# A graph layer's edge sum on one core: part of its products in two float32r parts, a 123rd row in the rank product, compares earlier

## The chip, the core and the metric

The kernel runs on one core of a Trainium2 chip. A core has a matrix engine (TensorE, PE in the profile, with its weight loads as PEld), VectorE (DVE), ScalarE (ACT), GpSimd (POOL), a queue engine SyncE (SP) that issues most transfers, and 16 DMA engines. The metric is the device time of one execution in microseconds; several executions were timed, and one more was profiled.

## The reference

A message sum over 206250 edges into 6250 nodes, a small three-layer network on each node, a residual and a layer norm. Rows have 128 float32 values.

```python
edge_aggr = jnp.zeros((n, 128)).at[src].add(edge_attr_128)       # 206250 rows into 6250
combined  = concatenate([x, edge_aggr, global_expand], -1) @ W_c + b_c
h = softplus(combined @ W1 + b1)
h = softplus(h @ W2 + b2)
out = layernorm(x + h @ W3 + b3)
```

`src` is random, so the sum is the work: each edge's row has to find its node. The sums must keep float32 accuracy; the one-hot operands of the products below are exact zeros and ones.

## The kernel before, in words

The nodes are cut into 32 buckets of 196 (`BL`). The edge rows are sorted by bucket on the chip and then summed bucket by bucket. There are eight groups of edge columns (`GROUPS`, 846 pairs of columns in all); groups 5, 6 and 7 (from `GAP` on) are called late here, and their positions are worked out in two parts.

1. *Rows.* `load_rows` (SP, `sync_dma` L293) brings 1032 KB of edge rows; `code_rows` (ACT L1114) writes a code beside each row.
2. *Positions* of a group: `count_set` (DVE L498) builds the one-hot tile `pair_ib` of the buckets of 16 columns; `counted`, `evened` and `started` make from it each bucket's first position for every four columns (a quad); `ranked` counts, for each row, the rows ahead of it: one matmul with `pair_ib` (L557, 122 rows contracted, 512 columns), and then, for each quad, a weight load and a matmul of `starts_h` (L559) that adds the bucket's start. In late groups the tile is `starts_h_late`. `slot_set` (DVE L576) takes the slot out of the result. `pair_set` and `paired` (L727, L742) give the row number in DRAM of each pair.
3. *Sort.* A piece is up to three pairs. `compare` builds its one-hot `sort_hot`: for every second piece on VectorE (L1137), for the others by six ACT operations (L1140) and a relu (L1142). `gather` (PE L1153) permutes the rows with it, fp32, 129 columns a matmul; `settle` (ACT L1165) copies PSUM into one of six `pair_sets`; `scatter_row` (POOL L1182) writes a pair of columns to the DRAM table `rows_by` with an indirect DMA, one every 1.3 us in the plan (`SCATTER`). SP also writes filler rows (`some`, the fills).
4. *Sum.* `sum_steps` reads `rows_by` back, up to eight chunks of 128 rows in a load (`chunks`, six buffers). A unit is up to four chunks of one load. `match` (DVE L990) builds the unit's one-hot `hot` (node within the bucket, 196 columns a chunk), `product` (PE L1013) multiplies it with the chunk, fp32, and `add` (DVE L1036) adds the finished PSUM part into `sums_t`.
5. *Nodes.* `node_layers` runs the network on blocks of 512 nodes (PE L1356, L1357, L1360, L1395; ACT L1367 to L1373; DVE L1381, L1403, L1406; POOL L1437). The sum steps that are left after the last gather run between its steps.

The order on PE, DVE, ACT and SP is written out by a planner inside the program: each step gets a planned time (`when`), and the sorted list is the program order of all four queues. `COMPARED`, `GATHERED`, `SETTLED` say how long ahead of a piece's first scatter its steps stand; `SPREAD` adds to that for a compare on ACT. GpSimd's scatters follow the same plan. The planned times only set the order; on the chip each instruction waits for its semaphores.

## Time and profile before

| | us |
|---|---|
| median of 3 runs (lowest, highest) | 1288.87 (1285.73, 1288.93) |
| profiled execution | 1289.92 |
| its span, first to last instruction | 1288.2 |
| mean granted TensorE clock | 0.962 |
| PE, DVE, ACT, POOL busy | 1167.7, 1027.6, 1003.9, 880.9 |
| scatters L1182, first start to last | 22.1 to 1127.0 |
| products L1013 busy | 675.1 |
| gathers L1153 busy | 498.5 |

A row of a group of instructions reads: line, engine, operation, output and input tiles, shapes, count; then busy us, mean ns of one, the idle time of its engine just ahead of them and what ended it. An fp32 matmul of the program shows as two records (L1013 has 3516 for 1758 matmuls). Durations of matmuls overlap in the pipeline, so busy time over count is below the mean of one. "issue" as a releaser is time in which the engine waited for nothing that the profile shows.

### The profile page before, as it was taken

The page shows a single profiled execution, that of the slowest core. Times are in us where ns is not written, and L with a number is a line of the kernel's source. Part 1 is how long each engine was busy: PE and PEld are TensorE (multiplying, and loading weights), DVE is VectorE, ACT ScalarE, POOL GpSimd, SP SyncE. Part 2 cuts the span into 40 slices and gives each one's busy share as a digit, 9 for nine tenths or more (in the row PEclk, how much of TensorE's full clock was granted, in tenths as well). Part 3 has the DMA queues.
Part 4 walks back from the last instruction along what each step waited for, and adds up shares of the span by engine and source line. Part 5 has one row for each costly group of instructions (what it writes and reads, how often), then busy time and mean ns, then how long its engine had stood idle before and what let it go on. Part 6 is the DMA issues. An engine that isn't in the chain of part 4 may idle for free.

```text
span 1288.2 us, 26304 instructions
## 1 busy us (share of the span) xinstructions
PE 1167.7 (91%) x8617; PEld 1111.8 (86%) x8617; DVE 1027.6 (80%) x2260; ACT 1003.9 (78%) x2335; POOL 880.9 (68%) x915
## 2 busy tenths in 40 slices
PE   5778898888998998999899999999999999899893
PEld 5667788877988898989899999999999999898772
DVE  7868977888789977899878887789876767687784
ACT  5897987899687888977998888988899999403343
POOL 2777777777577776776777777777777777750334
PEclk9788998989999998999999999999999999999996
DMA  6789998899999997997999999999999999874421
GB/s 248 240 296 347 344 334 288 305 344 355 339 327 331 362 330 278 319 325 246 322 309 309 323 336 328 345 313 335 316 350 334 369 336 363 288 218 140 140 75 53
DMA packets 174636, 381.96 MB, mean 297 GB/s; under 512 B 27546, under 2 KB 118626, under 8 KB 160670
## 3 DMA queue, kind: packets, MB, share of 16 engines
q1 hardware_dynamic: 130751, 260.70, 61.2%
q0 software_dynamic: 41328, 115.65, 23.1%
q10 hardware_dynamic: 2415, 3.85, 0.9%
q8 instruction: 72, 1.18, 0.4%
q14 instruction: 70, 0.57, 0.1%
HBM read 242.47 MB, written 142.20 MB: 299 GB/s over the span
## 4 chain that ended last, share of the span: by engine, by line
PE 65%; DVE 12%; ACT 8%; DMA 7%; issue 4%; POOL 3%; SPq 0%; ACTq 0%; DVEq 0%; POOLq 0%
PE part L1013 37%; PE sorted L1153 21%; ACT pairs L1165 4%; DMA rows_by<-pairs,pair 4%; POOL rows_by L1182 3%; ACT sort_hot L1140 3%; DMA chunks<-rows_by 3%; DVE hot L990 2%; DVE past L727 1%; PE small L557 1%; PE small L559 1%; ACT sort_hot L1142 1%; DVE sort_hot L1137 1%; DVE sums_t L1036 1%; PE small L1395 1%
## 5 line engine op out<-in xcount | busy, mean ns | idle before, releaser
L1182 POOL DMA_INDIRECT rows_by<-pairs,pair x846 | 828.1, 979 | 298.3 <-issue 202.8
L1013 PE MATMUL part<-hot,chunks 128*128 128x196 f32 x3516 | 675.1, 335 | 13.2 <-DVE sums_t L1036 9.9
L1165 ACT COPY pairs<-sorted 64x387 f32<-64x387 f32 (+2 forms) x1144 | 542.6, 474 | 118.8 <-PE sorted L1153 95.7
L1013 PEld LDWEIGHTS part<-hot,chunks 128*128 128x128 f32 x3516 | 582.0, 193 | 21.9 <-DVE sums_t L1036 11.3
L1153 PE MATMUL sorted<-rows,sort_hot 122*128 122x129 f32 x3384 | 498.5, 288 | 44.5 <-ACT sort_hot L1142 32.0
L1153 PEld LDWEIGHTS sorted<-rows,sort_hot 122*128 122x128 f32 x3384 | 457.6, 199 | 53.5 <-ACT sort_hot L1142 36.3
L990 DVE TENSOR_TENSOR hot<-chunks,both_ps 128x784 f32<-128x784 f32 (+3 forms) x541 | 426.1, 809 | 9.2 <-DMA chunks<-rows_by 9.0
L1140 ACT ACTIVATE sort_hot<-plain,slot 122x128 f32<-122x128 f32 x840 | 292.8, 394 | 18.6 <-PE sorted L1153 6.3
L1036 DVE TENSOR_TENSOR sums_t<-sums_t,part 128x392 f32<-128x392 f32 (+1 forms) x262 | 143.5, 548 | 134.0 <-PE part L1013 133.0
L1137 DVE TENSOR_TENSOR sort_hot<-slot,both_ps 122x768 f32<-122x768 f32 x143 | 134.5, 940 | 1.9 <-PE sorted L1153 1.0
L1142 ACT ACTIVATE sort_hot<-sort_hot 122x768 f32<-122x768 f32 x143 | 118.6, 830 | 3.9
L1437 POOL TENSOR_SCALAR y<-y,mv,rs 128x128 f32<-128x128 f32 x40 | 31.1, 785 | 93.8 <-DVE rs L1425 93.5
L576 DVE TENSOR_REDUCE slot<-small 122x16 f32<-122x512 f32 (+2 forms) x109 | 72.9, 668 | 21.5 <-PE small L559 20.7
L1367 ACT ACTIVATE away<-sorted,z_bias 128x512 f32<-128x512 f32 (+2 forms) x13 | 8.5, 656 | 72.9 <-PE sorted L1357 72.9
L498 DVE TENSOR_TENSOR pair_ib<-pair_block,plain 122x512 bf16<-122x512 bf16 (+2 forms) x157 | 63.4, 411 | 0.2
L557 PE MATMUL small<-pair_ib,half 122*122 122x512 bf16 (+2 forms) x109 | 43.3, 398 | 7.6 <-DVE slot L576 7.5
L742 PEld LDWEIGHTS <-past 128*128 128x128 f16 x424 | 25.4, 100 | 17.9 <-DVE past L727 12.7
L727 DVE TENSOR_TENSOR past<-both_ps,starts 128x512 f16<-128x512 f32 (+1 forms) x61 | 39.8, 664 | 1.2 <-PE small L742 0.9
L742 PE MATMUL small<-jump,past 128*128 128x56 f16 (+3 forms) x424 | 29.4, 190 | 11.8 <-DVE past L727 8.4
L559 PEld LDWEIGHTS <-starts_h 128*122 128x122 bf16 x236 | 25.3, 148 | 11.9 <-issue 7.7
L1114 ACT COPY rows<-pair_i 122x16 f32<-122x16 f32 x106 | 22.2, 209 | 17.0 <-DMA rows<-in_edge 16.4
L727 DVE TENSOR_TENSOR past<-both_ps,starts_late 128x512 f16<-128x512 f32 (+2 forms) x49 | 32.3, 661 | 0.0
(163 smaller groups left out, 515.6 us busy)
## 6 DMA issues: line engine op xcount, KB each, us to landing
rows<-in_edge SPq DMA_DIRECT2D x105, 1032.0 KB
chunks<-rows_by SPq DMA_DIRECT2D x362, 136.0 KB
chunks<-rows_by SPq DMA_DIRECT2D x203, 204.0 KB
chunks<-rows_by SPq DMA_DIRECT2D x75, 272.0 KB
rows_by<-pairs,pair POOLq DMA_INDIRECT x846
rows_by<-fill SPq DMA_DIRECT2D x10, 1249.5 KB
rows_by<-fill SPq DMA_DIRECT2D x10, 714.0 KB
chunks<-rows_by SPq DMA_DIRECT2D x13, 408.0 KB
```

Of the source, the lines that this page charges most:

```text
L498: nc.vector.tensor_tensor(ib, cols.unsqueeze(2).to_broadcast([PN, m, SB, QUAD]), bucket_at[:PN].unsqueeze(1).to_broadcast([PN, m, SB, QUAD ...
L576: nc.vector.tensor_reduce(to, of, axis=mybir.AxisListType.X, op=ALU.max)
L727: nc.vector.tensor_tensor(past[:, :, a:b], twice_ps[:KB].unsqueeze(1).unsqueeze(1).to_broadcast([KB, 2, b - a, P // 2]), own["starts"][:, ...
L990: nc.vector.tensor_tensor(hot[:, q - a:q - a + m], chunks[j][:, lo:hi + 1:step, D:W].to_broadcast([P, m, BL]), iota_ps.unsqueeze(1).to_bro ...
L1013: nc.tensor.matmul(part[:, b - base_of[v], :], t[:, place_in(j, q), :D], hot[:, q - a], start=first, stop=last)
L1036: nc.vector.tensor_add(here, here, of)
L1137: return [lambda: nc.vector.tensor_tensor(hot[:PN, :2 * m], slot[:PN, at:at + 2 * m].unsqueeze(2).to_broadcast([PN, 2 * m, P]), slot_ps[:P ...
L1140: return [lambda j=j: nc.scalar.activation(hot[:PN, j], by_slot[:PN], AF.Abs, bias=slot[:PN, at + j:at + j + 1], scale=-1.0) for j in rang ...
L1142: for j in range(2 * m)] + [lambda: nc.scalar.activation(hot[:PN, :2 * m], hot[:PN, :2 * m], AF.Relu, bias=1.0, scale=-1.0)]
L1153: nc.tensor.matmul(out[:, j, :], hot[:PN, at], rows_at[col // LOAD_COLS][:PN, col % LOAD_COLS, :], start=True, stop=True)
L1165: nc.scalar.copy(sets_at[i][64 * n:64 * n + 64, lo:lo + m, h, :W], out[64 * h:64 * h + 64, :m, :])
L1182: s = nc.gpsimd.indirect_dma_start(out=dst, out_offset=bass.IndirectOffsetOnAxis(ap=at, axis=0), in_=rows[:, j].rearrange("p a b -> p (a b ...
```

## The change

Four things change together.

- *Fine units.* From planned time 650 us on, every fourth unit of three or four chunks (every third after the last gather) is "fine", if its chunks stand at even steps in their load. ScalarE casts the unit's rows to a float32r tile `high` (one buffer); VectorE writes the rows less `high` back over the rows as float32r (`low`); TensorE then does two float32r matmuls a chunk, with `high` and with the rest, in place of one fp32 matmul. 81 units with 284 chunks become fine: 54 units with 189 chunks ahead of the last gather, 27 with 95 behind it. The `hot` tile becomes float32r (other units read it as float32), with five buffers instead of six.
- *A 123rd row.* In late groups the buckets' starts are made once more as rows (a small matmul in `evened`, a cast in `started`), stored to a DRAM tile `starts{g}`, and read back one row per 16 columns into the 123rd partition of `pair_ib` (`starts_row`). The rank matmul contracts 123 rows, and the 187 pairs of weight load and matmul with `starts_h_late` go. SP issues 12 stores and 47 row loads for it.
- *Compares ahead.* `SPREAD` goes from 2.0 to 4.5 planned us, and `sort_hot` has four buffers instead of three.
- *Smaller fills.* A fill DMA covers at most 3 rows of 136 values a partition instead of 7: some 40 more DMAs with the same bytes.

```diff
-FILL, DUE = 7, 8
+FILL, DUE = 3, 8
-SHARE, SPREAD = 2, 2.0
+SHARE, SPREAD = 2, 4.5
+FINE_FROM, FINE_EVERY = 650.0, (4, 3)
-    t["rank"] = MARK * (k == f) + (f > k)
+    t["rank"] = MARK * (k == f) + (f > k) + (k == PN)
+    rows_of = {g: dram.tile([2 * (s1 - s0) // QUAD, KB], BF16, name=f"starts{g}")
+               for g, (s0, s1) in enumerate(groups) if g >= GAP}
-    hots = ctx.enter_context(tc.tile_pool(name="hots", bufs=6))
+    hots = ctx.enter_context(tc.tile_pool(name="hots", bufs=5))
-        sort_p = phase.enter_context(tc.tile_pool(name="sort", bufs=3))
+        sort_p = phase.enter_context(tc.tile_pool(name="sort", bufs=4))
...
+                if split:
+                    nc.tensor.matmul(small_of["counts", ts][:n, P:P + KB], own["evens"][:, at],
+                                     lower_h, start=True, stop=True)
...
+                rows_h = per.tile([BATCH * STEP // QUAD, KB], BF16, name="starts_rows", bufs=2)
+                nc.vector.tensor_copy(rows_h[:n], small_of["counts", ts][:n, P:P + KB])
+                sync_dma(rows_of[g][at], rows_h[:n])
+
+            def starts_row(t):
+                q0, n = t // QUAD, per_set(t)
+                sync_dma(in_set[t][PN:PN + 1].rearrange("p q b c -> p (q b c)"),
+                         rows_of[g][q0:q0 + n].rearrange("(o q) k -> o (q k)", o=1))
...
-                nc.tensor.matmul(pr, rank_h, in_set.pop(t)[:, :, :NB, :], start=True, stop=False)
+                k = PN + split
+                nc.tensor.matmul(pr, rank_h[:k], in_set.pop(t)[:k, :, :NB, :], start=True, stop=split)
+                if split:
+                    return
...
                     at_step(4 * n, (6, lambda t=t: count_set(t)))
+                    at_step(4 * n, (7, lambda t=t: starts_row(t)))
                     rank(n, 4 * n + APART, t)
...
+            def high(n):
+                high_of[n] = sums_p.tile([P, HALF, D], F32R, name="high", bufs=1)
+                for to, at, m in runs_of(n):
+                    nc.scalar.copy(high_of[n][:, to], chunks[units_of[n][0]][:, at, :D])
+
+            def low(n):
+                for to, at, m in runs_of(n):
+                    rows = chunks[units_of[n][0]][:, at, :D]
+                    nc.vector.tensor_tensor(rows.bitcast(F32R), rows, high_of[n][:, to].bitcast(F32),
+                                            op=ALU.subtract)
...
+                    if n in fine:
+                        nc.tensor.matmul(part[:, b - base_of[v], :], high_of[n][:, q - a], by,
+                                         start=first, stop=False)
+                        nc.tensor.matmul(part[:, b - base_of[v], :], rows.bitcast(F32R), by,
+                                         start=False, stop=last)
...
+                since += 1
+                if product_at[n] > FINE_FROM and since >= FINE_EVERY[product_at[n] > ends[-1]] and e - a > 2 and len(runs_of(n)) == 1:
+                    since = 0
+                    fine.add(n)
+                    found.append((match_at[n], len(found), lambda n=n: high(n)))
+                    found.append((max(match_at[n] + 1.0, product_at[n] - 1.5), len(found), lambda n=n: low(n)))
```

The change moves instructions. Below are rows of the written order; the line numbers of the changed program are its own (L1062 and L1064 are the two float32r products, L1067 the fp32 product, L1213 the gather, L1225 the settle, L1200 and L1202 the compare on ACT, L584 the rank matmul, L1027 `hot`, L1040 `low`, L1090 the add).

TensorE, around the rank matmul of one set of 16 columns in a late group. Before:

```order
L1013 MATMUL part<-hot,chunks 128x196 x4
L557 LDWEIGHTS half
L557 MATMUL small<-pair_ib,half 122x512
L559 LDWEIGHTS starts_h_late
L559 MATMUL small<-half,starts_h_late 122x128
L559 LDWEIGHTS starts_h_late
L559 MATMUL small<-half,starts_h_late 122x128
L559 LDWEIGHTS starts_h_late
L559 MATMUL small<-half,starts_h_late 122x128
L559 LDWEIGHTS starts_h_late
L559 MATMUL small<-half,starts_h_late 122x128
L1153 MATMUL sorted<-rows,sort_hot 128x129 x3
```

After:

```order
L1062 MATMUL part<-hot,high 128x196
L1064 MATMUL part<-hot,chunks 128x196
L1062 MATMUL part<-hot,high 128x196
L1064 MATMUL part<-hot,chunks 128x196
L584 LDWEIGHTS half
L584 MATMUL small<-pair_ib,half 122x512
L1213 MATMUL sorted<-rows,sort_hot 128x129 x3
L1067 MATMUL part<-hot,chunks 128x196 x3
```

The four pairs behind the rank matmul are gone, and the unit ahead of it is a fine one here: two matmuls a chunk instead of one.

ScalarE, where it compares one piece between the copies of others, at about 306 us of the profiled span. Before:

```order
L1165 COPY pairs_112<-sorted 64x3x129 x4
L1140 ACTIVATE sort_hot<-plain,slot 122x128 x2
L1165 COPY pairs_113<-sorted 64x3x129 x2
L1140 ACTIVATE sort_hot<-plain,slot 122x128 x3
L1165 COPY pairs_113<-sorted 64x3x129 x2
L1140 ACTIVATE sort_hot<-plain,slot 122x128
L1142 ACTIVATE sort_hot<-sort_hot 122x768
L1165 COPY pairs_108<-sorted 64x3x129 x4
```

After (the buffers are numbered three higher: 111 here is 108 there):

```order
L1225 COPY pairs_115<-sorted 64x3x129 x2
L1200 ACTIVATE sort_hot<-plain,slot 122x128 x3
L1225 COPY pairs_115<-sorted 64x3x129 x2
L1200 ACTIVATE sort_hot<-plain,slot 122x128 x3
L1225 COPY pairs_116<-sorted 64x3x129 x2
L1202 ACTIVATE sort_hot<-sort_hot 122x768
L1225 COPY pairs_116<-sorted 64x3x129 x2
L1225 COPY pairs_111<-sorted 64x3x129 x2
```

The last operation of the compare (the relu) stood behind both copies of the second half of 113 before; now two copies of the same buffer (116) come after it.

VectorE, among the sum steps behind the last gather. Before:

```order
L1036 TENSOR_TENSOR sums_t<-sums_t,part 128x392
L990 TENSOR_TENSOR hot<-chunks,both_ps 128x784 x2
L990 TENSOR_TENSOR hot<-chunks,both_ps 128x392
L1036 TENSOR_TENSOR sums_t<-sums_t,part 128x392
L990 TENSOR_TENSOR hot<-chunks,both_ps 128x392 x2
```

After:

```order
L1090 TENSOR_TENSOR sums_t<-sums_t,part 128x392
L1027 TENSOR_TENSOR hot<-chunks,both_ps 128x784 x2
L1040 TENSOR_TENSOR chunks<-chunks,high 128x4x128
L1027 TENSOR_TENSOR hot<-chunks,both_ps 128x392
L1090 TENSOR_TENSOR sums_t<-sums_t,part 128x392
L1027 TENSOR_TENSOR hot<-chunks,both_ps 128x392 x2
```

A `low` of four chunks stands between the one-hots; the adds behind it come that much later on VectorE's queue.

More of the change, by code (lines that the diff above doesn't have):

```diff
@@ L8 @@
 F32 = mybir.dt.float32
+F32R = mybir.dt.float32r
 BF16 = mybir.dt.bfloat16
@@ L432, in doubtful @@
                               key=lambda e: (e[0] * e[1], -e[0]))
-                assert k <= FILL and lo + rows * k <= end
+                assert lo + rows * k <= end
                 return lo, rows, k
@@ L482, in opened @@
                     own["starts"] = per.tile([KB, 2, Q_MAX], F32, name="starts" + late, bufs=max(2, deep))
-                    own["starts_h"] = per.tile([KB, Q_MAX], BF16, name="starts_h" + late, bufs=deep)
+                    if not split:
+                        own["starts_h"] = per.tile([KB, Q_MAX], BF16, name="starts_h", bufs=1)
                     own["earlier"] = per.tile([KB, 2, Q_MAX], F32, name="earlier" + late, bufs=deep)
@@ L977, in place_in, with runs_of @@
                 return mixed[0] + 2 * (c - all_of[mixed[0]][2]) + of - 1
-            def match(n):
+            def runs_of(n):
                 j, a, e = units_of[n]
-                hot = hots.tile([P, HALF, BL], F32, name="hot")
-                hots_of[n] = hot
-                q = a
+                q, found = a, []
                 while q < e:
@@ L1012, in product @@
                     last = met[v].count(b) == in_visit[v].count(b)
-                    nc.tensor.matmul(part[:, b - base_of[v], :], t[:, place_in(j, q), :D], hot[:, q - a],
-                                     start=first, stop=last)
+                    rows, by = t[:, place_in(j, q), :D], hot[:, q - a]
+                    if n in fine:
[3 more added lines that the diff above has]
+                                         start=False, stop=last)
+                    else:
+                        nc.tensor.matmul(part[:, b - base_of[v], :], rows, by.bitcast(F32),
+                                         start=first, stop=last)
                 if n == last_unit[j]:
@@ L1040, in sum_steps @@
             found, load_at, match_at, product_at, freed, at = [], {}, [], {}, {}, 0.0
-            opened = -1
+            opened, fine, since = -1, set(), 0
             for n, (j, a, e) in enumerate(units_of):
```

50 lines of the change are left out of this document (33 added, 17 removed).

## The prediction

> **What bounds the kernel now.** I read the page's busy shares and the chain first, then cut the span into the stages of the program and read busy times and waits stage by stage.
>
> ```profile
> span 1288.2 us, 26304 instructions
> PE 1167.7 (91%) x8617; PEld 1111.8 (86%) x8617; DVE 1027.6 (80%) x2260; ACT 1003.9 (78%) x2335; POOL 880.9 (68%) x915
> PE 65%; DVE 12%; ACT 8%; DMA 7%; issue 4%; POOL 3%; SPq 0%; ACTq 0%; DVEq 0%; POOLq 0%
> ```
>
> By these lines TensorE is the bound: 91% busy, 65% of the chain. By stages it looks different. Columns: the window, its length, then busy us (and instructions) of PE, PEld, DVE, ACT and POOL, the granted clock, the DMA share and GB/s. The second fence holds the product line L1013 alone (PE and PEld), the third the matmuls with `starts_h_late`.
>
> ```profile
> 0.00:640.00 640.00, 553.79 (x4418) 525.78 (x4418) 536.34 (x1354) 529.83 (x1249) 457.36 (x470) 0.95 0.89 314
> 640.00:1128.00 488.00, 481.92 (x3528) 475.72 (x3528) 374.31 (x624) 421.23 (x992) 371.78 (x382) 1.00 0.96 330
> 1128.00:1184.00 56.00, 55.84 (x300) 51.26 (x300) 44.31 (x78) 9.73 (x15) 15.47 (x16) 0.97 0.63 184
> 1184.00:1257.00 73.00, 66.02 (x333) 52.40 (x333) 58.41 (x146) 31.78 (x52) 22.17 (x30) 1.00 0.36 107
> ```
> ```profile
> 1128.00:1184.00 56.00, 48.39 (x274) 47.16 (x274) 0.97 0.63 184
> 1184.00:1257.00 73.00, 39.18 (x218) 36.33 (x219) 1.00 0.36 107
> ```
> ```profile
> 0.00:640.00 640.00, 6.19 (x64) 6.11 (x64) 1.96 (x12) 0.95 0.89 314
> 640.00:1128.00 488.00, 12.10 (x123) 11.84 (x123) 0.00 (x0) 1.00 0.96 330
> ```
>
> From 640 to 1128 us TensorE is 481.92 of 488 us busy. But GpSimd's scatters in the same stretch run without a gap. The first two rows are the scatter line L1182 before and after 640 us (minimum, median and maximum ns, first and last start); the next two are the first and the last scatter; then GpSimd's waits in 640:1105, and three kinds of its waits in 24:640 (total us, times, longest).
>
> ```profile
> L1182 POOL DMA_INDIRECT rows_by<-pairs,pair x465: 971/972/1407, 22.1 to 639.3; - x155
> L1182 POOL DMA_INDIRECT rows_by<-pairs,pair x382: 972/972/1168, 639.3 to 1127.0; - x191
> 22.14 1.22 POOL L1182 DMA_INDIRECT rows_by<-pairs,pair  x1 [20.50 <-DVE much L642]
> 1127.05 0.97 POOL L1182 DMA_INDIRECT rows_by<-pairs,pair  x1 [0.30 <-issue]
> POOL rows_by L1182 <- issue: 83.9, 275, 0.3
> POOL rows_by L1182 <- ACT pairs L1165: 7.0, 23, 0.3
> ```
> ```profile
> POOL rows_by L1182 <- DMA rows_by<-pairs,pair: 19.9, 35, 6.4
> POOL rows_by L1182 <- ACT pairs L1165: 16.9, 28, 2.1
> POOL rows_by L1182 <- ACT sort_hot L1140: 4.5, 11, 1.5
> ```
>
> After 640 us no wait is longer than 0.3 us, whatever its name: that is the gap that every scatter has. The cadence is (1127.05 − 639.3)/381 = 1.280 us; duration and gap alone give 0.972 + 0.305 = 1.277. So here **GpSimd's 846 scatters set the pace**, and TensorE, though full, keeps up. Before 640 us the cadence is (639.3 − 22.14)/464 = 1.330, which loses 464 × 0.052 = 24 us against the floor. Of it, waits beyond 0.3 us each are 9.4 us (scatters still in flight), 8.5 us (settled pairs) and 1.2 us (one-hots). After 1128 us the scatters are over: 1128:1184 is TensorE's (55.84 of 56), 1184:1257 alternates between TensorE (66.0 of 73) and VectorE (58.4).
>
> **The change, part by part.** The prices come from these rows: two pieces of the chain, then groups of one shape (busy us, mean ns, idle before).
>
> ```profile
> 1103.39 1.34 PE sorted L1153 x12
> 1104.73 1.33 PE part L1013 x8
> ```
> ```profile
> L559 PE MATMUL small<-half,starts_h_late 128*122 128x128 bf16 x187 | 18.3, 218 | 0.0
> L557 PE MATMUL small<-pair_ib,half 122*122 122x512 bf16 x103 | 41.6, 404 | 7.4 <-DVE slot L576 7.2
> L1165 ACT COPY pairs<-sorted 64x387 f32<-64x387 f32 x1116 | 534.4, 479 | 116.8 <-PE sorted L1153 94.1 <-DMA rows_by<-pairs,pair 3.3 <-PE part L1013 2.6
> L1368 ACT ACTIVATE away<-away 128x512 f32<-128x512 f32 x22 | 13.9, 630 | 0.7
> L1036 DVE TENSOR_TENSOR sums_t<-sums_t,part 128x392 f32<-128x392 f32 x248 | 138.5, 559 | 127.0 <-PE part L1013 126.0
> L1403 DVE TENSOR_TENSOR y<-small,x_sb 128x512 f32<-128x512 f32 x11 | 7.6, 691 | 16.8 <-PE small L1395 16.8
> ```
>
> *One float32r matmul.* An fp32 chunk is two records of 1.33/8 = 0.167 us, so 0.333 us for 196 columns. No row shows float32r. Lower bound: the column price of bf16, (404 − 218)/384 = 0.48 ns, times 196 is 0.095 us. Upper bound: a whole fp32 chunk, 0.333 us; that end is a rival below. I take 0.112 us, an fp32 record of 129 columns (1.34/12), in which a weight load of the same size already fits; it lies nearest to the lower end, and the bf16 pairs of L559 (18.3/187 = 0.098 with their loads) stand beside it. A chunk in two parts costs 0.224 us and saves **0.109 us**.
>
> [...]
>
> *Fine units in 640:1128.* 189 chunks in 54 units. TensorE: −189 × 0.109 = −20.6 us. ScalarE's cast (`high`) reads and writes 384 or 512 columns: 0.52 us (nearest L1165's 387 columns, 0.479) or 0.63 (L1368), mean 0.577: 54 × 0.577 = +31.2, so 421.2 becomes 452.4 of 488 (93%). VectorE's difference (`low`), between 0.55 and 0.69 us, mean 0.62: +33.5, 374.3 becomes 407.8. None of it lies on GpSimd's path as long as ScalarE's copies L1165 are not late: bounds 0 and, in a rival, +18. I take **0**.
>
> *The 123rd row.* 187 pairs of weights and matmul go: 6.19 us of TensorE before 640 (with DVE 1.96 for their casts, which return as the new ones) and 12.10 after. With the products that takes TensorE to 481.9 − 20.6 − 12.1 = 449 of 488 us: slack, no gain in this stage, since the scatters beside it are at their floor. In exchange SP issues 12 stores and 47 one-row loads, each ahead of its rank matmul by three planned steps. A row of the queue's waits shows what they can stand behind, in 560:1128:
>
> ```profile
> SPq L293 <- PE part L1013: 253.5, 117, 7.1
> SPq L293 <- PE sorted L1153: 32.8, 12, 14.0
> ```
>
> A row load behind a chunk load that waits 7.1 us for its buffer comes that much later. The order gives a row 9 to 12 us in groups 6 and 7, 2 to 18 in group 5, so a few rank matmuls will hold TensorE for some us, and the gathers queued behind them; the 39 us of slack cover it. If that cover were gone, 47 × 1 us would be the price. I take 0.
>
> *Compares 2.5 us earlier (SPREAD, one more `sort` buffer).* Columns: total us, times, longest.
>
> ```profile
> PE sorted L1153 <- ACT sort_hot L1142: 32.0, 23, 2.2
> ACT pairs L1165 <- PE sorted L1153: 33.1, 61, 1.7
> ```
>
> The first row is TensorE in 0:640: 32.0 us in 23 places where a gather waits for its one-hot from ScalarE, mostly 1 to 2 us, less than the 2.5 us by which the compare now stands earlier. Most of the 32 us should go. (The second, ScalarE in 640:1105, shows copies that wait for gathers; they are late by design there and cost GpSimd nothing.) What GpSimd gets of it is at most its 8.5 + 1.2 us of waiting for pairs and one-hots, about half of that, with a little from the 6.19 us of L559 that go near 570 to 640 us: **−5 us**, bounds 0 and −20 (all its waits, the lanes' 9.4 too, which the smaller fills could ease).
>
> *Smaller fills.* Same bytes in some 40 more DMAs of SP: between −9.4 (above) and +2; 0.
>
> *Fine units after the scatters.* (274 + 218)/2 = 246 chunks stand after 1128, a third of them fine in the new order (95 of 287 after the last gather): 81. In 1128:1184 TensorE loses 45 × 0.109 = 4.9 us, to 50.9; VectorE gains 13 × 0.62 = 8.0, to 52.3, and is now the longer: 56 becomes about 53. In 1184:1257 TensorE falls to 62.1 and VectorE rises by 10 × 0.62 to 64.8 of 73: two engines that hand each other work, so nothing gained. **−3 us**, bounds −9 (TensorE's saving in full) and +6 (VectorE's second half in full).
>
> Sum: 1289.92 (the profiled execution) − 5 − 3 = 1281.9; the median of the runs shown is 1.05 lower, so **1281**. A difference of 0.3% (3.9 us) is about what a measurement of this kernel tells from none.
>
> **Rivals.**
> 1. *The head clears* (chance 0.15). GpSimd's waits for pairs and for lanes both go (−15) and the parts are cheap enough for −6 in the tail: 1289 − 21 = 1268. For it: 32 us of TensorE's waits are exactly what moves. Against: 9.4 us of the waits are DMAs.
> 2. *Nothing arrives* (0.16). Scatters pace everything until 1127, the head's losses sit in DMAs, the tail gives to VectorE what TensorE saves: 1288.
> 3. *ScalarE takes over the pace* (0.12). In 640:1128 it has 66.8 us idle; 54 casts, each holding the queue for a late chunk or for the single `high` buffer, delay the copies L1165 behind them. It decides when a cast costs over 66.8/54 = 1.24 us; with 1.0 us of waiting each, 54 × 1.58 = 85: 85 − 67 = +18, and with the head's −5 and the tail's −3 that is 1299. Against: by the order a cast stands 3 us or more behind its chunk's landing.
> 4. *float32r is as slow as fp32* (0.08): 0.333 us a part, +0.333 a chunk. TensorE in 640:1128 becomes 481.9 − 12.1 + 63 = 533 (+45), the tail +15 and +12, the head −5: about 1356. Against: nothing but the bf16 rows.
> 5. *VectorE's `low` holds the scatters* (0.07). Its two operands lie in SBUF, from which GpSimd reads its row numbers at the same time. If each of the 54 meets one scatter and stretches it to the longest seen in that stage, 1168 instead of 972 ns, that is 54 × 0.2 = +11, and with −8 elsewhere 1292. For it: the other VectorE operations of that stage mostly have an operand in PSUM. Against: L498, two SBUF operands, and a median of 972.
>
> ```profile
> L498 DVE TENSOR_TENSOR pair_ib<-pair_block,plain 122x512 bf16<-122x512 bf16 x149 | 61.1, 419 | 0.2
> ```
>
> On the last, the Trainium skill ("SBUF — State Buffer", Who interferes with whom) names a VectorE operation with two SBUF inputs as one that contends with GpSimd reading SBUF. The trace, with a cadence of 1.280 beside such operations, does not show it; it does not rule it out for longer ones.
>
> **How the numbers follow.** Forecast 0.42 (own range 1274 to 1286), rivals 0.15, 0.16, 0.12, 0.08, 0.07. Leaving out rival 4 and the far ends of 1 and 3, about 0.2, the range is 1265 to 1300. Faster: most of the forecast (0.38) and rival 1 (0.15): 0.53. Within: rest of the forecast, rivals 2 and 5: 0.25. Slower: rivals 3 and 4 and a little of 5: 0.22.
>
> **What would show it.** Right: GpSimd's cadence before 640 us falls below 1.330 while the later one stays 1.28; TensorE's 32.0 us on L1142's successor shrink to under 10; TensorE busy near 449 in the steady stage; float32r records near 0.11 us; VectorE the busiest in 1128:1184. Wrong: waits of scatters above 0.3 us after 640, ScalarE over 97% there, rank matmuls waiting for a DMA, float32r records of 0.167 or more, scatters above 972 ns beside `low`.

## The result: slower by 2.7%

The changed kernel takes 1324.55 us (median of 6 runs, 1313.49 to 1325.01) where the kernel before takes 1288.78 (6 runs, 1285.73 to 1288.97): a ratio of **1.0268, interval 1.0234 to 1.0301**. Faster was forecast, with 1281 us and a range of 1265 to 1300; the time lies outside the range on the side of the slower rivals. The profiled execution took 1322.03 us, so against the 1289.92 of before 32.1 us have to be found. Three sets of the kernels below ran where the kernel before itself takes 1597 to 1623 us; each kernel is compared with the kernel before of its own set.

The head of the page and the stages of the changed kernel, cut at the same times as before (columns as there):

```profile
span 1320.3 us, 26370 instructions
PE 1143.4 (87%) x8442; PEld 1073.5 (81%) x8442; DVE 1081.2 (82%) x2341; ACT 1022.3 (77%) x2416; POOL 889.1 (67%) x915
PE 39%; DMA 20%; DVE 17%; ACT 11%; issue 6%; POOL 3%; SPq 2%; ACTq 0%; DVEq 0%; POOLq 0%
...
0.00:640.00 640.00, 544.77 (x4346) 510.99 (x4347) 532.28 (x1350) 514.12 (x1243) 455.63 (x467) 0.96 0.90 312
640.00:1128.00 488.00, 461.22 (x3379) 448.67 (x3377) 398.00 (x671) 442.62 (x1056) 368.65 (x373) 0.98 0.94 323
1128.00:1184.00 56.00, 35.54 (x191) 33.40 (x191) 46.92 (x59) 5.14 (x9) 27.08 (x27) 0.82 0.58 189
```

TensorE is busy for 24 us less and its share of the chain fell from 65% to 39%: it was relieved, and the time grew on the others. In 1128:1184, where it was busy 55.84 us of 56, it is busy 35.54.

Since GpSimd's 846 scatters pace the program, I take them as a clock: the start of the n-th scatter (counted from 0), less that of the n-th scatter of the kernel before, in us. Behind it stands the tail, from the start of the last scatter to the end of the span. The rows below `after`, the changed kernel, are kernels of the experiments; each row is one profiled execution.

```
scatter no.          100    200    250    300    350    475    550    650    725    845   tail
before                 0      0      0      0      0      0      0      0      0      0  161.1
after                0.9   -0.1   -7.2   -0.4    3.6    3.3    4.8    5.1   11.9   14.6  178.7
u_spread             0.6   -1.1   -7.7    0.3    3.0    1.7    3.1    4.0   12.4   13.3  185.7
u_noadd              1.0   -0.6   -9.0    0.2    2.2    2.0    3.4    4.6    8.4   10.2  164.9
u_tail               1.1    0.0   -6.9   -3.0    1.2    1.5    3.1    4.0    6.6    8.6  160.6
e_store              0.9   -1.0  -10.0   -2.2    0.0   -1.3    0.0    1.4   10.2   10.7  182.0
u_row                0.8   -0.5  -10.1   -8.3   -6.5   -8.4   -8.1   -7.1   -6.2   -5.0  184.1
e_ahead              0.9   -0.7   -8.2   -7.1   -5.3   -7.4   -7.5   -7.3   -7.2   -7.2  161.9
e_steady             0.9    0.7   -6.4   -4.0   -2.5   -5.0   -4.1   -2.6   -1.6    0.0  160.0
e_late               1.1   -1.1   -7.8   -7.7   -5.9   -8.2   -8.6   -8.4   -8.2   -8.2  166.1
```

So of the 32.1 us, 14.6 had been lost when the last scatter started, and 17.5 came in the tail. Each has its rows.

**The tail.** The chain of waits of the changed kernel behind the last scatter, and the timelines of VectorE and GpSimd there (start us, us, instruction):

```profile
1144.56 0.97 DVE hot L1027
1145.53 12.70 DVE chunks L1040
1158.27 0.53 PE part L1064
```
```profile
1145.44 12.77 DVE L1040 TENSOR_TENSOR chunks<-chunks,high 128x512 fp32r<-128x512 f32 x1
...
1142.68 15.85 POOL L1516 TENSOR_TENSOR x_sb<-x_sb,b_all 128x512 f32<-128x512 f32 x15
```

One `low` takes 12.77 us instead of 0.69. It ends at 1158.21, as the last of GpSimd's 15 additions of the bias to x runs out (1158.53). It had nothing to wait for by then: it had started.

**The waits before that.** TensorE's in 640:1143 (first row), SP's and ScalarE's before 640 us:

```profile
PE small L584 <- DMA pair_ib<-starts: 15.1, 10, 7.2
...
SPq L297 <- DVE pair_ib L506: 51.6, 8, 11.3
...
ACT rows L1174 <- DMA rows<-in_edge: 20.6, 7, 5.8
```

The rank matmuls wait 15.1 us for the row that comes back from DRAM. The longest of these waits reaches GpSimd: 7 us later a scatter has to wait for its settled pair (TensorE, then GpSimd).

```profile
895.84 0.68 PE L584 MATMUL small<-pair_ib,half 123*122 123x512 bf16 x1 [7.22 <-DMA pair_ib<-starts]
...
903.13 0.97 POOL L1242 DMA_INDIRECT rows_by<-pairs,pair  x1 [3.71 <-ACT pairs L1225]
```

Before 640 us it is the stores. SP stands 51.6 us at the stores of the starts, which VectorE has not yet made (7 of the 12 are issued within 0.1 us of the end of the cast that makes them); behind them are the loads of rows, and ScalarE's `code_rows` waits for those, 20.6 us (12.9 before).

### The profile page after: what moved, and what is told of

Its sections match the earlier page's. It is cut to its first block, busy times and chain, and to the rows that moved or that the text cites. A ratio compares the mean times of both kernels' runs of the same rounds, so it can differ in the third digit from the quotient of the medians.

```text
span 1320.3 us, 26370 instructions
## 1 busy us (share of the span) xinstructions
PE 1143.4 (87%) x8442; PEld 1073.5 (81%) x8442; DVE 1081.2 (82%) x2341; ACT 1022.3 (77%) x2416; POOL 889.1 (67%) x915
## 4 chain that ended last, share of the span: by engine, by line
PE 39%; DMA 20%; DVE 17%; ACT 11%; issue 6%; POOL 3%; SPq 2%; ACTq 0%; DVEq 0%; POOLq 0%
PE part L1067 19%; PE sorted L1213 12%; DMA chunks<-rows_by 8%; DMA rows_by<-pairs,pair 6%; ACT pairs L1225 6%; DMA pair_ib<-starts 4%; DVE hot L1027 4%; POOL rows_by L1242 3%; ACT sort_hot L1200 3%; SPq L297 2%; PE part L1064 2%; DVE past L756 2%; DMA rows<-in_edge 2%; DVE chunks L1040 2%; PE part L1062 1%
## 5 line engine op out<-in xcount | busy, mean ns | idle before, releaser
L1225 ACT COPY pairs<-sorted 64x387 f32<-64x387 f32 (+2 forms) x1144 | 543.6, 475 | 129.9 <-PE sorted L1213 88.2
L1067 PE MATMUL part<-hot,chunks 128*128 128x196 f32 x2948 | 578.8, 339 | 11.4 <-DVE hot L1027 6.0
L1213 PE MATMUL sorted<-rows,sort_hot 122*128 122x129 f32 x3384 | 494.7, 285 | 43.4 <-ACT pairs L1225 33.5
L1067 PEld LDWEIGHTS part<-hot,chunks 128*128 128x128 f32 x2948 | 495.3, 195 | 19.7 <-DVE hot L1027 5.7
L1213 PEld LDWEIGHTS sorted<-rows,sort_hot 122*128 122x128 f32 x3384 | 449.0, 196 | 63.1 <-ACT pairs L1225 54.6
L1027 DVE TENSOR_TENSOR hot<-chunks,both_ps 128x784 f32<-128x784 f32 (+5 forms) x541 | 427.8, 810 | 16.3 <-DMA chunks<-rows_by 13.1
L1200 ACT ACTIVATE sort_hot<-plain,slot 122x128 f32<-122x128 f32 x840 | 281.0, 392 | 9.4 <-DVE slot L605 5.9
L1090 DVE TENSOR_TENSOR sums_t<-sums_t,part 128x392 f32<-128x392 f32 (+1 forms) x262 | 143.3, 547 | 114.3 <-PE part L1067 106.2
L1035 ACT CAST high<-chunks 128x512 fp32r<-128x512 f32 (+1 forms) x81 | 45.4, 560 | 97.6 <-PE part L1062 80.1
L1202 ACT ACTIVATE sort_hot<-sort_hot 122x768 f32<-122x768 f32 x143 | 118.4, 828 | 0.4
L1064 PE MATMUL part<-hot,chunks 128*128 128x196 f32 x284 | 71.3, 286 | 27.9 <-DVE chunks L1040 27.6
L1062 PE MATMUL part<-hot,high 128*128 128x196 f32 x284 | 78.4, 307 | 6.3 <-ACT high L1035 3.4
L1064 PEld LDWEIGHTS part<-hot,chunks 128*128 128x128 f32 x284 | 55.6, 196 | 33.4 <-DVE chunks L1040 31.4
L584 PE MATMUL small<-pair_ib,half 122*122 122x512 bf16 (+4 forms) x109 | 43.4, 398 | 26.6 <-DMA pair_ib<-starts 16.9
L1040 DVE TENSOR_TENSOR chunks<-chunks,high 128x512 fp32r<-128x512 f32 (+1 forms) x81 | 62.3, 769 | 4.9 <-ACT high L1035 4.9
L1062 PEld LDWEIGHTS part<-hot,high 128*128 128x128 f32 x284 | 55.5, 195 | 9.0 <-issue 4.9
```

Of the source, the lines that this page charges most:

```text
L1027: nc.vector.tensor_tensor((hot if n in fine else hot.bitcast(F32))[:, to], chunks[j][:, at, D:W].to_broadcast([P, m, BL]), iota_ps.unsquee ...
L1040: nc.vector.tensor_tensor(rows.bitcast(F32R), rows, high_of[n][:, to].bitcast(F32), op=ALU.subtract)
L1062: nc.tensor.matmul(part[:, b - base_of[v], :], high_of[n][:, q - a], by, start=first, stop=False)
L1064: nc.tensor.matmul(part[:, b - base_of[v], :], rows.bitcast(F32R), by, start=False, stop=last)
L1067: nc.tensor.matmul(part[:, b - base_of[v], :], rows, by.bitcast(F32), start=first, stop=last)
L1090: nc.vector.tensor_add(here, here, of)
```

## The experiments

**Undoing one thing at a time.** Four kernels, each the changed one with one part out.

`u_noadd`, the additions of the last bias left out (the output lacks that bias):

```diff
-                for lo, hi, r in blocks_of(w):
-                    nc.gpsimd.tensor_tensor(
-                        x_of[n0][:r, lo:hi, :], x_of[n0][:r, lo:hi, :],
-                        b3_all[:r].unsqueeze(1).to_broadcast([r, hi - lo, D]), op=ALU.add)
```

> The changed kernel without GpSimd's 15 additions of the last bias to x (L1516); that bias is left out of the output. Lock theory (GpSimd's additions keep the first VectorE difference with two SBUF operands from ending until they are done): no difference of the tail is longer than 0.8 us (12.77 now), TensorE's 12.3 us wait for it is gone, the time falls by about 12 to 1311 (1308 to 1315). Rival (the tail is long because ScalarE's casts and VectorE's differences are too much for it, the 12.77 us is a wait that some other engine ends): the wait stays or goes elsewhere, the time falls by less than 4.

Measured: 1306.44 us (1303.45 to 1316.3), ratio to before 1.0164 (1.0115 to 1.0213). The group of all 81 differences, minimum, median and maximum ns:

```profile
L1040 DVE TENSOR_TENSOR chunks<-chunks,high x81: 543/654/693, 666.2 to 1263.1; 128x512 fp32r<-128x512 f32 x41, 128x384 fp32r<-128x384 f32 x40
```

No difference is longer than 0.69 us, and the tail falls from 178.7 to 164.9. **GpSimd's additions held it.** The median falls by 18, more than the 12 expected, since the scatters too were 4 us earlier in this run; the tail alone gives 13.8. The same happened in seven other profiled kernels: 15.89 us in `u_row`, 11.53 in `u_spread`, 14.96 in `e_store`, and 12.59, 13.47, 9.01 and 12.06 in `c_steady`, `d_steady`, `u_store` and `d_store`. In one, `f_end`, it did not; the last section has its rows.

```profile
1122.70 15.89 DVE L1027 TENSOR_TENSOR chunks<-chunks,high 128x512 fp32r<-128x512 f32 x1
...
1123.10 15.79 POOL L1503 TENSOR_TENSOR x_sb<-x_sb,b_all 128x512 f32<-128x512 f32 x15
```

These are the rows of `u_row`: the difference started before the first addition, and ends 0.3 us before the last one does.

`u_tail`, no fine unit behind the last gather:

```diff
-FINE_FROM, FINE_EVERY = 650.0, (4, 3)
+FINE_FROM, FINE_EVERY = 650.0, (4, 10 ** 6)
```

> The changed kernel with no fine unit behind the last gather (54 of 81 stay). Lock theory: no two-operand difference meets the additions except the few that run late from before the last gather; the stretch from the last scatter to the end, 178.7 us now, goes back to the 161 us of the kernel before: time about 1307 (1304 to 1311). Rival (the tail's fine units are worth 9 us of TensorE and only the wait is bad): the stretch stays above 166 us, time above 1311.

Measured: 1301.69 us (1298.11 to 1305.62), 1.0113 (1.0085 to 1.0141), below the 1304 to 1311 expected, since the last scatter too was 6.0 us earlier than in the changed kernel. The trace has 58 differences, not 54, since the edit tells the units apart by their planned times: 23 units go. The tail is 160.6 us, that of before; TensorE is busy again:

```profile
1136.00:1192.00 56.00, 55.84 (x299) 51.42 (x298) 43.95 (x77) 9.74 (x15) 16.08 (x16) 0.96 0.61 183
```

All of the 17.5 us went with these 23 units, 13.8 of it by the additions (`u_noadd`). The rival of this run is refuted.

`u_row`, the starts of the late groups added by the weight loads and matmuls again (the edit puts all places of the diff on `starts_rows`, `starts_row` and the rank matmul back; three are shown):

```diff
-                    at_step(4 * n, (7, lambda t=t: starts_row(t)))
-                sync_dma(rows_of[g][at], rows_h[:n])
-                k = PN + split
-                nc.tensor.matmul(pr, rank_h[:k], in_set.pop(t)[:k, :, :NB, :], start=True, stop=split)
-                if split:
-                    return
+                nc.tensor.matmul(pr, rank_h[:PN], in_set.pop(t)[:PN, :, :NB, :], start=True, stop=False)
```

> The changed kernel with the starts of the late groups added by the 187 weight loads and matmuls again, without the stores and the row loads. Row theory (rank matmuls wait for the row that comes back from DRAM, gathers and scatters stand behind them): TensorE's 15 us of waits for pair_ib<-starts after 640 us are gone, the lag of the scatters against the kernel before, +3.3 us at scatter 475 and +11.9 at 725, grows by no more than 4 in that stretch, time about 1317 (1314 to 1320). Rival (casts on ScalarE make the settled pairs late there): the lag still grows by 7 or more, time 1322 or above, with TensorE 12 us busier.

Measured: 1310.31 us (1307.9 to 1319.19), 1.0193 (1.0151 to 1.0234), 14 below the changed kernel where 7 were expected. The last scatter is 5.0 us ahead of the kernel before instead of 14.6 behind. From 475 to 725 the lag grows by 2.2, not by 8.6: the rank matmuls' waits were most of that. (In the other kernels with the row it grows by 5.1 to 11.5, in `e_steady`, without it, by 3.4.) But 11.7 of the 19.6 us had been lost by scatter 475, where I had expected nothing: the row theory named only half of what the row costs. `e_store` below is on the other half.

`u_spread`, the compares at their old place:

```diff
-SHARE, SPREAD = 2, 4.5
+SHARE, SPREAD = 2, 2.0
-        sort_p = phase.enter_context(tc.tile_pool(name="sort", bufs=4))
+        sort_p = phase.enter_context(tc.tile_pool(name="sort", bufs=3))
```

> The changed kernel with the compares at their old place (SPREAD 2.0, three sort buffers). Theory 1 (the earlier compares on ScalarE delay the copies that scatters wait for): the scatters' waits for settled pairs before 640 us fall from 35.3 to about 17 us, the one-hot waits of TensorE come back (32 us), the lag at scatter 475 falls from +3.3 to about 0, time about 1321. Theory 2 (the smaller fills make row loads late on SP's queue): ScalarE's waits for rows, 24.4 us before 640, stay, the lag stays at +3 or more, time 1324 or above.

Measured: 1330.88 us (1321.74 to 1336.09), 1.0327 (1.027 to 1.0385). Neither theory came out whole. The lag at scatter 475 is 1.7 against 3.3, the last scatter 1.3 earlier; what is longer is the tail (185.7), and why stays open. The scatters' waits for settled pairs before 640 us fall from 35.3 to 29.1 us, not to 17. TensorE's waits in 0:640, first with the old place, then with the new:

```profile
PE sorted L1213 <- ACT sort_hot L1202: 28.4, 23, 2.2
PE sorted L1213 <- ACT pairs L1225: 11.2, 9, 3.6
```
```profile
PE sorted L1213 <- ACT pairs L1225: 28.3, 38, 3.7
...
PE sorted L1213 <- ACT sort_hot L1202: 3.6, 1, 3.6
```

Earlier compares change the name of the wait: 28.4 us for one-hots and 11.2 for copies become 28.3 for copies. The same ScalarE does both, and GpSimd, which waits for the copies, is not earlier for it.

**Parts alone, on the kernel before.** Three kernels without the 123rd row, with the compares ahead and the smaller fills: without fine units (`e_ahead`), with the 58 ahead of the last gather (`e_steady`), and with the 15 that stand planned 50 us or more behind it (`e_late`).

```diff
-FINE_FROM, FINE_EVERY = 650.0, (4, 3)
+FINE_FROM, FINE_EVERY = 650.0, (10 ** 6, 10 ** 6)      # e_ahead
+FINE_FROM, FINE_EVERY = 650.0, (4, 10 ** 6)            # e_steady
...
+                if ... and product_at[n] > ends[-1] + 50.0 and ...    # e_late
```

> The changed kernel without the 123rd row and without fine units (compares ahead and smaller fills over the kernel before), on a chip on which the kernel before takes its usual time. Theory of separate causes: 8 us ahead of the kernel before at scatter 475 and at the last, tail 161, 1280 (1277 to 1284). Rival (the wait is only shifted): last scatter within 3 us of before, 1286 to 1290.

> That kernel with the 54 fine units ahead of the last gather. Theory of separate causes: some 5 us above e_ahead, by scatters stretched beside differences with two SBUF operands, and more if one of them meets the additions behind the last scatter. Rival (fine units cost nothing ahead of the last gather): within 2 us of e_ahead.

> That kernel with fine units only from planned 50 us behind the last gather on, after GpSimd's additions. Lock theory: no difference longer than 0.8 us, tail 161 give or take 3, within 3 us of e_ahead. Rival (the tail's fine units cost, lock or not): tail 164 or more, 4 us or more above e_ahead.

Measured, against 1288.11 us of before: `e_ahead` 1283.79 us, **0.9972 (0.9958 to 0.9985)**; `e_steady` 1285.61, 0.9979 (0.9960 to 0.9999); `e_late` 1284.95, 0.9971 (0.9957 to 0.9984).

`e_ahead` keeps its 7 us from scatter 250 to the last, as expected, and has the lowest median of all kernels here, if by 4.3 us and not by 8; `e_late` and `e_steady` are not separated from it. In `e_steady` the 5.0 us that it is ahead at scatter 475 have shrunk to 0.0 at the last: 5.0 us for 58 fine units (in `u_row` it is 3.4). That is what the stretched scatters come to: after 640 us the 66 scatters that ran beside one of the differences lasted 5.28 us longer in all than 66 times 0.972, the 311 others 0.87. It is the order of starts that tells: 29 scatters started while a difference ran, and 22 of them took over 1.0 us; of the 37 that were running when a difference started, one did. One of the pairs, in the changed kernel:

```profile
1067.51 0.69 DVE L1040 TENSOR_TENSOR chunks<-chunks,high 128x512 fp32r<-128x512 f32 x1
...
1067.62 1.42 POOL L1242 DMA_INDIRECT rows_by<-pairs,pair  x1 [0.30 <-DVE hot L1027]
1069.35 0.97 POOL L1242 DMA_INDIRECT rows_by<-pairs,pair  x1 [0.30 <-issue]
```

This scatter, which starts beside a difference, takes 1.42 us instead of 0.97, and no later one makes up for it, because GpSimd is at its floor. In time `e_steady` is 1.8 us above `e_ahead`, which the intervals do not separate.

In `e_late` no difference is longer than 0.69 us, and still its profiled tail is 166.1 us against 161.9. First `e_ahead`, then `e_late`, the two stages behind the last scatter:

```profile
1120.00:1176.00 56.00, 54.57 (x295) 50.48 (x296) 44.96 (x78) 9.73 (x15) 16.23 (x16) 0.97 0.63 185
1176.00:1249.00 73.00, 65.69 (x330) 51.67 (x330) 58.28 (x143) 30.55 (x51) 22.17 (x30) 1.00 0.38 114
```
```profile
1119.00:1175.00 56.00, 52.37 (x283) 48.15 (x284) 48.36 (x83) 13.34 (x21) 16.23 (x16) 0.94 0.61 182
1175.00:1248.00 73.00, 62.89 (x320) 48.40 (x320) 60.27 (x140) 31.73 (x54) 23.22 (x30) 0.95 0.38 115
...
PE part L1051 <- DVE chunks L1027: 6.9, 4, 2.5
...
ACT high L1022 <- PE part L1049: 32.6, 10, 6.2
```

TensorE waits 6.9 us for the differences, and ScalarE stands 32.6 us until the single `high` buffer is free. So there is a second, small cost of fine units in the tail, some 4 us in the profiled execution; two further pairs of profiles show it too (tails of 175.4 us in `c_late` against 171.5 in `c_ahead`, 175.7 in `d_late` against 171.1 in `d_ahead`). In the timed runs (1.2 us between the medians, the same ratio) it is not separated from none.

**The stores of the starts.** `e_store` issues each store six planned steps later, behind the cast it waits for:

```diff
-                sync_dma(rows_of[g][at], rows_h[:n])
+                to_store[ts] = rows_h
...
+                if split:
+                    at_step(base + gap + 5 * APART, (5, lambda ts=ts: store(ts)))
```

> The changed kernel with the 12 stores six planned steps later. Store theory: SP's waits ended by VectorE's pair_ib before 640 us fall from 51.6 below 15, the lag at scatter 475 goes from +3.3 to -5 or below, TensorE's waits for the rows read back stay near 15 us, time about 1316. Rival (the row loads do the harm): the lag at 475 stays above 0.

Measured: 1320.78 us (1319.74 to 1325.4), 1.0262 (1.0232 to 1.0292). SP's waits before 640 us that VectorE ends with `pair_ib`:

```profile
SPq L297 <- DVE pair_ib L506: 26.8, 6, 7.4
```

They fall from 51.6 to 26.8, not below 15, and the lag at scatter 475 goes from +3.3 to −1.3, not to −5. Half of the waits gone, 4.6 of the 10.7 us between the changed kernel and `e_ahead` back. The loads of edge rows on SP say the same. Against `e_ahead` the one at 285 us starts 5.8 us late in the changed kernel, and those from 454 to 610 us start 10 to 16 us late; in `e_store` 5.9 and 4 to 8, and in `u_row`, without stores, none behind 285 us is more than 1 us late. The first group's four stores stand at 260, 269, 275 and 287 us. The loss from scatter 650 to 725 stays, 8.8 us. The loads of the starts' rows cannot have caused the early part: the first is issued at 568 us, at scatter 409, and by scatter 350 the changed kernel is already 10.1 us behind `u_row`. `f_end` was to settle the rest, with each store a whole batch later:

> The changed kernel with each of the 12 stores one batch (21 planned steps) later than the cast that it waits for. Store theory: no wait of SP before 640 us is ended by VectorE's pair_ib any more, the loads of rows are within 2 us of e_ahead's through 500 us, the lag at scatter 475 goes from +3.3 to -6 or below; the loss from 650 to 725 by the rows read back, 7 to 9 us, stays. Rival (half of the loss is something else that comes with the 123rd row): the lag at 475 stays at -2 or above, as with six steps.

It ran where the kernel before takes 1623.41 us (1642.68 us, 1.0143, 1.0082 to 1.0203), and SP still stood 36.6 us there, up to 800 us, in waits ended by `pair_ib`. So that all of the loss before 640 us is the stores' stays likely and not shown.

**Which of the two parts gains in `e_ahead`.** `f_fill` is the kernel before with `FILL` 3:

> The kernel before with the smaller fills alone. Fill theory (the 7 us that e_ahead gains lie at scatter 200 to 250, where the kernel before loses 6.05 us in one wait for scatters in flight, and the run with the compares at their old place gains them too): the scatters are 6 us or more ahead at number 250 and 4 or more at the last, time 1283 (1281 to 1286). Compare theory (the gain is the compares'): less than 3 us ahead at the last, time within 2 us of the kernel before.

It too ran there: 1626.0 against 1623.41, 1.0019 (0.9984 to 1.0053). Nothing can be read from it. What speaks for the fills is `u_spread`, which has the old compares and is 7.7 us ahead at scatter 250 all the same; the kernel before loses 6.05 us in one wait for scatters in flight there, at 340 us, where the kernels of the table with the smaller fills have none above 2.8. That is argued from these profiles, not shown by a run of its own; and of the kernel before there is one profile, so whether it has this wait each time is not known.

**Where the kernel before takes 1598 us.** The same kernels as `e_ahead`, `e_steady`, `e_late` and `e_store`, in two earlier sets. The first:

> The changed kernel without the 123rd row and without any fine unit: compares ahead and smaller fills are left, over the kernel before. Theory of separate causes (the earlier compares gain some 8 us before 640 us, which the row's stores took back; the differences with two SBUF operands stretch the scatters afterwards): the scatters are 8 us ahead of the kernel before at number 475 and stay so to the last, no scatter after 640 is stretched, the end is 161 us behind the last: 1280 (1277 to 1284), faster than before. Rival (compares ahead only shift the wait; the 8 us come back in the later groups): last scatter within 3 us of before, 1286 to 1290.

> The changed kernel without the 123rd row and without fine units behind the last gather; the 54 ahead of it stay. Theory of separate causes: 8 us ahead at scatter 475; the 54 differences stretch scatters that start beside them by some 5 us in all, so 3 us ahead at the last; tail 161: 1285 (1282 to 1288), some 5 above the run without any fine unit. Rival (the fine units cost nothing before the last gather): as that run, within 2 us.

> The changed kernel without the 123rd row and with fine units only well behind the last gather (planned 50 us after it), so that none runs while GpSimd adds the bias. Lock theory: no difference is longer than 0.8 us, the scatters stay 8 us ahead to the last; the tail is 161 us give or take 3, as TensorE saves up to 6 us there and VectorE takes as much: 1280 (1277 to 1284). Rival (fine units in the tail cost by ScalarE's single buffer and its queue, lock or not): the tail is 164 or more, 1284 or above.

> The changed kernel, with the 12 stores of the starts six planned steps later, behind the cast they wait for; everything else stays. Store theory (a store that waits for VectorE's cast holds SP's queue, the loads of rows behind it come late): SP's waits that VectorE ends with pair_ib, 51.6 us in 8 before 640 us, fall below 15; ScalarE's waits for rows, 20.6 us, fall below 8; the lag of the scatters at number 475 goes from +3.3 to -5 or below; the waits of TensorE for the rows read back stay near 15 us; time about 1316. Rival (the row loads, not the stores, do the harm): the lag at 475 stays above 0.

Measured, against 1597.51 us: `c_ahead` 1.0043 (1.0016 to 1.0071), `c_steady` 1.0070 (1.0033 to 1.0107), `c_late` 1.0068 (1.0030 to 1.0106), `u_store` 1.0112 (1.0078 to 1.0145). The second set:

> c_ahead again, since on the chip of that call the kernel before itself took 1597 us: no 123rd row, no fine unit, compares ahead and smaller fills left. Theory of separate causes: scatters 8 us ahead of the kernel before at number 475 and at the last, tail 161, 1280 (1277 to 1284). Rival: the last scatter within 3 us of before, 1286 to 1290.

> c_steady again for the same reason: the 54 fine units ahead of the last gather stay. Theory of separate causes: some 5 us above d_ahead, by stretched scatters. Rival: within 2 us of d_ahead.

> c_late again for the same reason: fine units only from planned 50 us behind the last gather on. Lock theory: no difference is longer than 0.8 us, the tail is 161 give or take 3, the time within 3 us of d_ahead. Rival (the tail's fine units cost, lock or not): the tail is 164 or more, 4 us or more above d_ahead.

> u_store again for the same reason: the changed kernel with the 12 stores six planned steps later. Store theory: SP's waits ended by VectorE's pair_ib before 640 us fall from 51.6 below 15, the lag at scatter 475 goes from +3.3 to -5 or below, time about 1316. Rival (the row loads do the harm): the lag at 475 stays above 0.

Measured, against 1597.95 us: `d_ahead` 1.0048 (1.0015 to 1.0082), `d_steady` 1.0033 (0.9994 to 1.0073), `d_late` 1.0050 (1.0018 to 1.0081), `d_store` 1.0176 (1.0123 to 1.0230). Of the part before the last scatter they tell nothing, since the scatters are some 300 us behind by other waits. Their tails do tell: one difference fell into the additions in `c_steady` and in `d_steady`, and the tails are 184.3 and 184.7 us against 171.5 and 171.1 without fine units. The gain of `e_ahead` is not there: in both sets it is a loss of half a percent. What lengthens all these kernels is not shown; `c_ahead` moves the same 382 MB as `e_ahead`, and its matmuls stand 121.6 us (2.2 in `e_ahead`) in waits that nothing in the profile ends.

## Why the prediction was wrong

By the scatter clock the 32.1 us are: −7.2 for fills and compares (`e_ahead`), +5 for fine units ahead of the last gather (`e_steady`), the rest of the 14.6, +17, for the 123rd row, and +17.5 in the tail. These shares are rough: the changed kernel, `u_noadd` and `u_tail`, which differ almost only in the tail, have their last scatter at 14.6, 10.2 and 8.6, so against `u_row` and `e_steady` the row comes out between 8.6 and 19.6. None of the rivals has this path. Three of the prediction's own signs of being wrong did show (scatters that wait up to 3.7 us after 640 us, rank matmuls that wait for a DMA, scatters above 972 ns beside `low`); the additions, which cost 13.8, were not among them.

- *What bounds the kernel.* Right: scatters pace it to 1127 us, TensorE's relief there gained nothing, and TensorE is below 95% busy in the steady stage now without the end coming nearer.
- *The price of a float32r matmul, 0.112 us.* Right: the 487 steps from one such matmul to the next within a unit have a median of 0.113 us. In the four-chunk unit at 695 us they lie between 0.108 and 0.114, but for the first, 0.175. The rival by which float32r is as slow as fp32 is refuted. The saving was smaller than the price says: TensorE's busy time fell by 24.3 us, half of the 49 that 284 × 0.109 and the 18.3 of the 187 pairs add up to, and in the steady stage to 461.22 us, not 449.
- *`high` and `low`, 0.577 and 0.62 us.* Right where nothing contends: `low` 0.55 and 0.69, `high` 0.507 and 0.612. ScalarE did not become the pace (442.62 of 488 us), against that rival.
- *"Fine units after the scatters, −3".* **The step that failed most.** It counted engine time, with +6 as its worst end, and measured +17.5. GpSimd's 15 additions were in the trace of before, 15 us long, from 1128.12 us on, and I did not ask what an operation with two SBUF operands does beside them. Rival 5 had the mechanism, and put it beside the scatters alone, priced at 11. (In the sum's VectorE term 58.4 + 10 × 0.62 is 64.6, not 64.8, which changes nothing; the units are 56 and 25 by the trace, not 54 and 27, with the chunks as stated.)

```profile
1128.12 15.46 POOL L1456 TENSOR_TENSOR x_sb<-x_sb,b_all 128x512 f32<-128x512 f32 x15
```

- *Rival 5, beside the scatters.* The forecast had 0 there, the rival 54 × 0.2 = 11 at the most; it measured 5.28, by few but longer stretches (up to 0.5 us). The median of 972 ns, my evidence against, could not show it: a median does not see 23 long scatters among 377. And the trace of before did show it beside L498, against what I wrote. After 640 us it has five scatters above 1.0 us, and four of them start while a `pair_ib` is being made (eight scatters do so in all). One of them, VectorE and then GpSimd:

```profile
823.58 0.42 DVE L498 TENSOR_TENSOR pair_ib<-pair_block,plain 122x512 bf16<-122x512 bf16 x1
...
823.70 1.15 POOL L1182 DMA_INDIRECT rows_by<-pairs,pair  x1 [0.31 <-issue]
```

- *"The 123rd row, 0: the 39 us of slack cover it."* Wrong twice. The rank matmuls' waits (15.1 us, one of 7.2) are less than the slack in sum, but each holds the gathers behind it, and ready pairs last a few us (the wait of 7.2 us came through to a scatter as 3.7): 8.6 us of scatters were lost from 475 to 725 that TensorE's idle time later could not return. And the 12 stores were counted, but not what they wait for. I priced the row loads by what stands ahead of them on SP, and did not price the loads that stand behind a store that waits for VectorE.
- *"Compares ahead, −5".* A gain of 7 is there (`e_ahead`), but hardly theirs: the 32.0 us of TensorE's waits went as forecast (3.6 left for L1202) and came back as waits for copies of the same engine. The smaller fills, which I had at 0, are the likelier cause.

## What to carry to other kernels

Before giving VectorE an operation with two operands in SBUF, look for GpSimd's work in the same stretch: a run of GpSimd operations can hold it until the run ends, and a pace-setting GpSimd is itself stretched. A DMA that waits for a computation belongs behind that computation in its queue, with all that stands behind it counted as late. An engine's slack in a stage does not cover a wait on it, if a pace-setter downstream holds only a few us of ready work.

## What the runs showed of the hardware that was not expected

A VectorE subtraction with both operands in SBUF can be held by GpSimd's additions until a whole run of them is nearly over: in eight profiles it lasted 9.0 to 15.9 us where 0.55 to 0.69 is its own time, through up to 15 additions of 0.4 to 1.3 us. In `u_row` it was so though its record starts 0.4 us before the first addition. The Trainium skill ("SBUF — State Buffer", Who interferes with whom) states that the shared port pair is an exclusive lock and that a VectorE instruction with two SBUF inputs contends with a GpSimd instruction that reads SBUF; the rows agree that the two contend, and add that the wait need not end with one addition.

It does not always go that way. In `f_end`, the first of three differences (first VectorE's, then GpSimd's rows) fell where additions waited for their loads, and ended between two of them after 1.25 us. The other two fell into an unbroken run of 12 additions and were done after 1.41 and 1.00 us all the same; two additions of that run took 1.60 and 1.72 us instead of 1.27.

```profile
1467.26 1.25 DVE L1051 TENSOR_TENSOR chunks<-chunks,high 128x384 fp32r<-128x384 f32 x1
...
1474.20 1.41 DVE L1051 TENSOR_TENSOR chunks<-chunks,high 128x384 fp32r<-128x384 f32 x1 [1.64 <-ACT high L1046]
...
1478.75 1.00 DVE L1051 TENSOR_TENSOR chunks<-chunks,high 128x512 fp32r<-128x512 f32 x1
...
1465.61 2.49 POOL L1527 TENSOR_TENSOR x_sb<-x_sb,b_all 128x512 f32<-128x512 f32 x2 [0.64 <-DMA x_sb<-in_x]
1468.81 1.27 POOL L1527 TENSOR_TENSOR x_sb<-x_sb,b_all 128x512 f32<-128x512 f32 x1 [0.71 <-DMA x_sb<-in_x]
1470.27 12.54 POOL L1527 TENSOR_TENSOR x_sb<-x_sb,b_all 128x512 f32<-128x512 f32 x12 [0.19 <-DMA x_sb<-in_x]
```

What decides between the two outcomes no run here shows. One of the six timed runs of the changed kernel was 11 us below the others (1313.49); whether it was one that got in is open, as only one run was profiled.
